# A ScalarE copy that reads PSUM in steps of four tokens and writes them side by side

## The chip, the cores and the metric

The kernel runs on one core of a Trainium2 chip. The metric is the time of one execution on the device, in microseconds (us). A core has five engines that run side by side and wait for each other through semaphores: TensorE (matrix products; in the profile "PE" for matmuls and "PEld" for weight loads, which overlap the matmuls), VectorE ("DVE"), ScalarE ("ACT"), GpSimd ("POOL") and SyncE ("SP", which here issues transfers). Matmuls write to PSUM; the other data lie in SBUF.

## The reference

The network has two layers on an input of shape (8, 256, 32, 32): 8 batches, 256 channels, 1024 tokens (32 x 32 pixels). Everything is fp32.

```
# layer 0: 8 heads of 64, softmax over the queries (axis 1)
xt   = x.reshape(B, C, S).transpose(0, 2, 1)
qkv  = (xt @ w_qkv + b_qkv).reshape(B, S, 8, 3 * 64); q, k, v = split(qkv)
attn = softmax(einsum('bihd,bjhd->bijh', q, k) * 64**-0.5, axis=1)
res  = einsum('bijh,bjhd->bihd', attn, v).reshape(B, S, 512)
t    = res @ w_out + b_out + xt
# layer 1
t = t + attention(layernorm(t), W)              # 1024 x 1024 scores per batch
t = t + top2_of_8_experts(layernorm(t), ...)    # two 256x256 matrices per expert, gelu between
```

The change concerns `res`, the result of layer 0's attention, and the product `res @ w_out`.

## The kernel before

The batches go through the two attentions one after the other. For seven of them the experts' rows are scattered to memory and worked off in blocks afterwards; the last batch goes through all experts densely.

Layer 0 (`layer0`) goes through steps (g, j): g is one of 4 pairs of heads (128 of the 512 inner channels), j one of 8 blocks of 128 keys. In each step TensorE makes scores for two heads (`score`, L468), VectorE takes their maximum (L483, L492), ScalarE takes the exponential and its sum (`soften`, L509), and TensorE multiplies with the values divided by the sums (`gather_values`, L545). It sums all 8 key blocks of a pair into two PSUM banks `po[0]` and `po[1]`, each 128 channels x 512 tokens. With the last key block ScalarE copies both to `res[:, g, :]` in SBUF (L563); `res` has 128 channels on the partitions, then 4 pairs, then 1024 tokens. So there are 8 copies in a batch and 64 in all, always two together. In the steps (0, 3), (1, 1) and (2, 1) TensorE also makes the next pair's queries and keys (`project_pair`, L350), which ScalarE evicts from PSUM (L315); the pair before is finished two steps late (`LAG = 2`), so the copies of pairs 0 and 1 fall beside projections. These copies stand ahead of the evictions L315 on ScalarE, and those of pair 2 ahead of an exp. The pool `ps_acc` has only two buffers, which `po`, `pr` and others take in turn: the next pair's first products wait until the copies have freed them.

After the last step comes the output product: for each of 8 blocks i of 128 tokens, four matmuls over the pairs g add up `pr` (L636), with `res` as the weights that are loaded and `wo` (128 x 256) as what moves; VectorE adds `pr` to the residual `t1` (L639) and the layer norm of layer 1 begins (L235, L236, L238 to L242). As the trace counts, each fp32 matmul is two records, each with its own weight load: 8 x 4 x 2 = 64 records of L636 in a batch, 512 in all. In front of this stage and behind it stand products for the next batch (L328, L387); layer 1's own attention has products of the same shape in L695 (`py`, weights `aT`).

The tokens of a block are not side by side. `NH2` = 2 halves of 512 tokens, each of `NB` = 4 blocks: block i holds the tokens 4p + i of its half, for p from 0 to 127, so that the partition p of a block's tile is the p-th group of four tokens. The function `own` picks a block out of `res` with this step of 4 elements (16 bytes).

The order of the instructions on each engine is set when the program is built, by the order of the code and by `tc.issue_after`; it is the same before and after the change.

Of the kernel before, what the change touches and what calls it, by code (L numbers as in the profile page):

```python
# [19 lines left out]
def kernel(  # L20
# [23 lines left out]
    nc = tc.nc  # L44
    P = 128
    B, C, S = x.shape
# [6 lines left out]
    NH2 = S // 512  # L53
    NPAIR = INNER // P
# [24 lines left out]
    def acc(name):  # L79

        return ps_acc.tile([P, 512], F32, tag="acc", name=name)
# [39 lines left out]
    wo = const.tile([P, NPAIR, C], F32, name="wo")  # L121
# [87 lines left out]
    NB = NT // NH2  # L209
    SQ = 32  # L210
    NQ = P // SQ

    def own(t, i):

        return t.rearrange("c (n p i) -> c n i p", n=NH2, i=NB)[:, i // NB, i % NB, :]

    def bcast(t, n):

# [222 lines left out]
    def layer0(b, xT, begun, routing, xs):  # L441
# [8 lines left out]
        res = one.tile([P, NPAIR, S], F32, tag="res", name=f"res_{b}")  # L450
# [8 lines left out]
        po, copied, counted = None, None, None  # L459
# [73 lines left out]
        def gather_values(at, turn):  # L533


            nonlocal po, copied
            g, j = steps[at]
            if j == 0 and turn == 0:
                po = [acc(f"po_{b}_{g}_{n}") for n in range(NH2)]
            past = dict(turned)  # L540
            for half in range(2):
                keys = ts(half, DK)
                n = (half + turn) % 2
                for h in range(2):
                    mm = nc.tensor.matmul(  # L545
                        po[n][ts(h, DK), :],
                        vss[at][keys, h, :],
                        exps[at, h][keys, ts(n, 512)],
                        start=(j == 0 and turn == 0),
                        stop=(j == NT - 1 and turn == 1),  # L550
                    )
                    if h == 0 and (j > 0 or turn > 0):
                        tc.add_manual_dep(mm.ins, past[1 - half].ins.name, BEHIND)

                turned[half] = relay.nop()
                tc.add_manual_dep(turned[half].ins, mm.ins.name, BEHIND)
            if turn == 0:
                return mm
            vss.pop(at)
            for h in range(2):  # L560
                exps.pop((at, h))
            if j == NT - 1:
                copied = [nc.scalar.copy(res[:, g, ts(n, 512)], po[n]) for n in range(NH2)]  # L563
            return mm

        last = len(steps) - 1
# [7 lines left out]
        for at in range(last + LAG + 1):  # L574
            g, j = steps[min(at, last)]
# [10 lines left out]
            if at >= LAG:  # L586
                with tc.issue_after(counted.ins) if counted else nullcontext():
                    gather_values(at - LAG, 0)
                counted = None
# [18 lines left out]
            if at >= LAG:  # L608
                array = gather_values(at - LAG, 1)
# [23 lines left out]
        for i in range(NT):  # L633
            pr = acc(f"pr_{b}_{i}")
            for g in range(NPAIR):
                nc.tensor.matmul(  # L636
                    pr[:, :C], own(res[:, g, :], i), wo[:, g, :], start=(g == 0), stop=(g == NPAIR - 1)
                )
            nc.vector.tensor_add(t1[:, i, :], pr[:, :C], t1[:, i, :])  # L639
        return t1  # L640
# [675 lines left out]
    for b in range(B):  # L1316
        xT = next_x
        if b + 1 < B:
            next_x = load_x(b + 1)
        if b > 0:  # L1320
            xs = load_squares(b)
        t1 = layer0(b, xT, begun, routing, xs)
        if b + 1 < B:
            begun = Begin(b + 1, next_x)
            t2 = attend(b, t1, begun.at)
            n2, _, l = normed(b, t2, begun.at)
            nc.sync.dma_start(groups[0].sums[b], t2)
            routing = dispatch(b, n2, l, groups[0])
            continue
        experts(groups[0])  # L1330
        others = Results(groups[0])
        others.begin()
        norm = None

        def fill(place):

            nonlocal norm
            others.tick(place)
            if place == "last products":
                norm = Norm(t1, one.tile([P, NT, D], F32, tag="xa", name=f"n2_{b}"), 1e-5, f"f{b}")  # L1340
                return norm.blocks(0, NT - 1)

        t2 = attend(b, t1, fill, others.tick)
        dense(b, t2, norm, others.tick)
        assert others.added == len(others.units) and not others.whole
# [42 lines left out]
```

## Time and profile before

| | us |
|---|---|
| runs of the kernel (three) | 2415.96, 2416.36, 2419.54 |
| median | 2416.36 |
| the profiled execution, its own time | 2397.03 |
| span in its profile (first to last instruction) | 2395.3 |
| TensorE matmuls busy, of the span | 2353.9 |
| ScalarE busy, of the span | 938.0 |
| L636 matmuls / weight loads, busy | 121.6 / 120.7 |
| L563 copies, busy | 34.2 |

The granted clock of TensorE was 0.996 of full speed. In the profile "L563" is a line of the kernel; a group of instructions is given as out<-in, with its shape (partitions x elements), its number, its busy time together, the mean ns of one, and the idle time of the engine just before with what ended it. Matmuls are pipelined, so the duration of a single one is longer than its share of the time; the distance from one start to the next says what it costs. Durations come from one profiled execution, which took 2397.03 us, 0.8% less than the median of the runs.

### The profile page before, as it was taken

The page shows a single profiled execution, that of the slowest core. Times are in us where ns is not written, and L with a number is a line of the kernel's source. Part 1 is how long each engine was busy: PE and PEld are TensorE (multiplying, and loading weights), DVE is VectorE, ACT ScalarE, POOL GpSimd, SP SyncE. Part 2 cuts the span into 40 slices and gives each one's busy share as a digit, 9 for nine tenths or more (in the row PEclk, how much of TensorE's full clock was granted, in tenths as well). Part 3 has the DMA queues.
Part 4 walks back from the last instruction along what each step waited for, and adds up shares of the span by engine and source line. Part 5 has one row for each costly group of instructions (what it writes and reads, how often), then busy time and mean ns, then how long its engine had stood idle before and what let it go on. Part 6 is the DMA issues. An engine that isn't in the chain of part 4 may idle for free.

```text
span 2395.3 us, 36813 instructions
## 1 busy us (share of the span) xinstructions
PE 2353.9 (98%) x13759; PEld 1313.9 (55%) x13759; DVE 1541.2 (64%) x3660; ACT 938.0 (39%) x1570; POOL 420.4 (18%) x391
## 2 busy tenths in 40 slices
PE   9999999999999999999999999999999999999898
PEld 3356534654466336633664356435653388887565
DVE  5775587457845785578647864787468763334776
ACT  3651266126611662156315641465136612221111
POOL 0000012000200020003000200020002234444663
PEclk9999999999999999999999999999999999999999
DMA  8993201010101010001000100100010256664454
GB/s 294 386 386 106 53 19 36 1 36 12 43 1 36 8 47 1 18 18 54 1 18 18 47 8 3 34 25 12 1 36 19 76 176 220 219 215 162 148 172 119
DMA packets 114778, 196.59 MB, mean 82 GB/s; under 512 B 15752, under 2 KB 58408, under 8 KB 112808
## 3 DMA queue, kind: packets, MB, share of 16 engines
q1 hardware_dynamic: 88504, 126.52, 16.0%
q0 software_dynamic: 25008, 67.20, 9.1%
q8 instruction: 109, 1.79, 0.3%
q10 hardware_dynamic: 1088, 0.52, 0.1%
q14 instruction: 69, 0.57, 0.1%
HBM read 108.88 MB, written 110.90 MB: 92 GB/s over the span
## 4 chain that ended last, share of the span: by engine, by line
PE 90%; DVE 5%; DMA 2%; ACT 1%; issue 1%; POOL 0%; SPq 0%; DVEq 0%; ACTq 0%; POOLq 0%
PE po L545 19%; PE psc L468 18%; PE py L695 8%; PE ps L670 7%; PE pqk L350 7%; PE pr L636 5%; PE pv L387 4%; PE ph L1025 4%; PE pe L1050 4%; PE pdh L1254 2%; PE px L655 2%; PE pdy L1278 2%; PE pa L689 2%; PE pqk L328 2%; PE px L1015 1%
## 5 line engine op out<-in xcount | busy, mean ns | idle before, releaser
L509 ACT ACTIVATE ex<-psc,nmax 128x1024 f32<-128x1024 f32 x512 | 570.5, 1115 | 304.1 <-DVE scrap L492 220.4
L468 PE MATMUL psc<-qk,qk 64*64 64x512 f32 x4096 | 577.4, 593 | 10.3 <-ACT ex L509 10.3
L545 PE MATMUL po<-ex,vs 64*64 64x512 f32 x4096 | 573.2, 592 | 1.3 <-DVE vs L525 0.3
L492 DVE TENSOR_SCALAR_CACHE_REDUCE scrap<-psc,nmax 128x512 f32<-128x512 f32 x512 | 384.5, 751 | 149.0 <-PE psc L468 121.8
L483 DVE TENSOR_REDUCE nmax<-psc 128x1 f32<-128x512 f32 x512 | 350.7, 685 | 9.3 <-PE psc L468 9.3
L468 PEld LDWEIGHTS psc<-qk,qk 64*64 64x64 f32 x4096 | 180.7, 132 | 285.9 <-ACT ex L509 138.3
L545 PEld LDWEIGHTS po<-ex,vs 64*64 64x64 f32 x4096 | 177.6, 132 | 273.0 <-issue 81.2
L695 PE MATMUL py<-n,aT 128*128 128x256 f32 x1024 | 236.3, 384 | 2.9 <-DVE aT L691 2.9
L670 PE MATMUL ps<-nT,xa 128*128 128x512 f32 x512 | 236.0, 592 | 0.0
L695 PEld LDWEIGHTS py<-n,aT 128*128 128x128 f32 x1024 | 190.5, 190 | 66.1 <-DVE aT L691 41.8
L888 POOL DMA_INDIRECT rows<-n,d_at x112 | 108.8, 972 | 654.4 <-DVE nmax L483 654.1
L681 ACT ACTIVATE ex<-ps,nmax 128x1024 f32<-128x1024 f32 x64 | 71.3, 1115 | 348.0 <-DVE nmax L678 333.5
L815 POOL TENSOR_TENSOR t<-t,n 128x2048 f32<-128x2048 f32 x8 | 36.3, 4532 | 924.0 <-DVE n L242 924.0
L350 PE MATMUL pqk<-xT,wqkv 128*128 128x512 f32 x384 | 171.2, 599 | 0.0
L701 DVE SCALAR_TENSOR_TENSOR t<-py,rs,t 128x256 f32<-128x256 f32 x64 | 30.9, 483 | 192.7 <-PE py L695 192.7
L670 PEld LDWEIGHTS ps<-nT,xa 128*128 128x128 f32 x512 | 93.5, 190 | 81.2 <-issue 75.1
L350 PEld LDWEIGHTS pqk<-xT,wqkv 128*128 128x128 f32 x384 | 71.0, 190 | 99.9 <-issue 77.8
L1134 POOL DMA_INDIRECT yk<-y,yat x112 | 111.0, 991 | 70.1 <-issue 27.1
L636 PEld LDWEIGHTS pr<-wo,res 128*128 128x128 f32 x512 | 120.7, 331 | 3.7 <-ACT res L563 3.7
L636 PE MATMUL pr<-wo,res 128*128 128x256 f32 x512 | 121.6, 398 | 0.3 <-ACT res L563 0.3
L387 PE MATMUL pv<-wqkv,xT 128*128 128x512 f32 x256 | 120.3, 599 | 1.2 <-DVE v L395 1.0
L315 ACT ACTIVATE qk<-pqk,b_qks 128x512 f32<-128x512 f32 x124 | 85.6, 691 | 88.9 <-PE pqk L350 79.8
(189 smaller groups left out, 2477.8 us busy)
## 6 DMA issues: line engine op xcount, KB each, us to landing
rows<-wb SPq DMA_DIRECT2D x7, 8192.0 KB, 51.7
y<-yb SPq DMA_DIRECT2D x63, 256.0 KB, 2.3
xs<-in_x_dram SPq DMA_DIRECT2D x64, 128.0 KB, 4.0
out_dram<-oT SPq DMA_DIRECT2D x60, 128.0 KB, 2.9
xT<-in_x_dram SPq DMA_DIRECT2D x7, 1024.0 KB, 4.8
sums<-t SPq DMA_DIRECT2D x7, 1024.0 KB, 3.9
o<-sums SPq DMA_DIRECT2D x7, 1024.0 KB
wpack<-in_L_ffn_w_dram SPq DMA_DIRECT2D x4, 1024.0 KB
```

Of the source, the lines that this page charges most:

```text
L350: mm = nc.tensor.matmul(pq[:, ts(n, 512)], wqkv[:, cc, t, ts(g, P)], xT[:, cc, ts(n, 512)], start=(cc == 0), stop=(cc == NCC - 1),)
L387: nc.tensor.matmul(pv, self.xT[:, cc, ts(i, P)], wqkv[:, cc, 2, :], start=(cc == 0), stop=(cc == NCC - 1),)
L468: mm = nc.tensor.matmul(pss[at, h][ts(c, DK), ts(n, 512)], k[r, j * P + c * DK : j * P + (c + 1) * DK], q[r, ts(n, 512)], start=True, stop ...
L483: firsts[at, h] = nc.vector.tensor_reduce(nmax, pss[at, h][:, ts(0, 512)], AX.X, ALU.max, negate=True)
L492: seconds[h] = nc.vector.tensor_scalar(scrap, pss[at, h][:, ts(1, 512)], -1.0, nmaxes[at, h], ALU.mult, ALU.min, accum_out=nmax,)
L509: nc.scalar.activation(ex, pss.pop((at, h)), AF.Exp, bias=nmaxes.pop((at, h)), scale=1.0, accum_out=sums[at][:, h : h + 1],)
L545: mm = nc.tensor.matmul(po[n][ts(h, DK), :], vss[at][keys, h, :], exps[at, h][keys, ts(n, 512)], start=(j == 0 and turn == 0), stop=(j == ...
L636: nc.tensor.matmul(pr[:, :C], own(res[:, g, :], i), wo[:, g, :], start=(g == 0), stop=(g == NPAIR - 1))
L670: nc.tensor.matmul(psc[:, ts(n, 512)], xa[:, ec, ts(i, P)], nT[:, ec, ts(n, 512)], start=(ec == 0), stop=(ec == NCC - 1),)
L695: nc.tensor.matmul(py[:, :D], aT[:, ts(m, P)], n1[:, m, :], start=(m == 0), stop=(m == NT - 1))
L888: scatter = nc.gpsimd.indirect_dma_start(out=view[:, :], out_offset=bass.IndirectOffsetOnAxis(ap=ats[k][:, i : i + 1], axis=0), in_=n2[:, ...
L1134: ins = nc.gpsimd.indirect_dma_start(out=self.slot(at)[:, k, :], out_offset=None, in_=self.group.y[:, :], in_offset=bass.IndirectOffsetOnAxis(
```

## The change

The copy out of PSUM reorders the tokens: it goes over the four blocks i of its half and for each over p, so it reads `po` with a step of 4 elements and writes each block's 128 tokens side by side in `res`. The output product then takes a contiguous slice, and `own` is gone. What is computed stays the same.

```diff
-    def own(t, i):
-
-        return t.rearrange("c (n p i) -> c n i p", n=NH2, i=NB)[:, i // NB, i % NB, :]
-
...
             if j == NT - 1:
-                copied = [nc.scalar.copy(res[:, g, ts(n, 512)], po[n]) for n in range(NH2)]
+
+                copied = [
+                    nc.scalar.copy(
+                        res[:, g, ts(n, 512)].rearrange("c (i p) -> c i p", i=NB),
+                        po[n].rearrange("c (p i) -> c i p", i=NB),
+                    )
+                    for n in range(NH2)
+                ]
             return mm
...
                 nc.tensor.matmul(
-                    pr[:, :C], own(res[:, g, :], i), wo[:, g, :], start=(g == 0), stop=(g == NPAIR - 1)
+                    pr[:, :C], res[:, g, ts(i, P)], wo[:, g, :], start=(g == 0), stop=(g == NPAIR - 1)
                 )
```

## The prediction

> **What bounds the kernel now.** I read the engine totals first, then the chain of waits, then the groups of instructions with their shapes kept apart, and last the timeline around each place where `res` is written and read. From the page:
>
> ```profile
> PE 2353.9 (98%) x13759; PEld 1313.9 (55%) x13759; DVE 1541.2 (64%) x3660; ACT 938.0 (39%) x1570; POOL 420.4 (18%) x391
> ...
> PE po L545 19%; PE psc L468 18%; PE py L695 8%; PE ps L670 7%; PE pqk L350 7%; PE pr L636 5%; PE pv L387 4%; PE ph L1025 4%; PE pe L1050 4%; PE pdh L1254 2%; PE px L655 2%; PE pdy L1278 2%; PE pa L689 2%; PE pqk L328 2%; PE px L1015 1%
> ```
>
> TensorE is on the chain 90% of the span, so a microsecond saved or lost on it counts in full unless a wait follows. The reader of `res`, L636, is 5% of the chain. ScalarE, which writes `res`, is only 39% busy. But share of busy time says little about where its lateness is felt. The groups by shape:
>
> ```profile
> L695 PEld LDWEIGHTS py<-n,aT 128*128 128x128 f32 x1024 | 190.5, 190 | 66.1 <-DVE aT L691 41.8 <-issue 0.2
> L636 PEld LDWEIGHTS pr<-wo,res 128*128 128x128 f32 x512 | 120.7, 331 | 3.7 <-ACT res L563 3.7
> L563 ACT COPY res<-po 128x512 f32<-128x512 f32 x64 | 34.2, 588 | 28.9 <-PE po L545 28.9
> ```
>
> The same weight load, 128 rows by 128 columns in fp32, takes 331 ns for `res` and 190 ns for `aT`. The only difference I find is the step between columns: `own` picks every fourth fp32 (16 bytes), `aT` is contiguous. A load overlaps a matmul, so its duration is not its price; the price is the distance from one matmul to the next. Timeline of both stages (columns: start us, length us):
>
> ```profile
> 168.50 15.09 PEld L636 LDWEIGHTS pr<-wo,res 128*128 128x128 f32 x64 [0.45 <-ACT res L563]
> 168.72 15.18 PE L636 MATMUL pr<-wo,res 128*128 128x256 f32 x64
> ...
> 183.73 1.88 PE L328 MATMUL pqk<-xT,wqkv 128*128 128x512 f32 x4
> ...
> 207.90 3.62 PE L695 MATMUL py<-n,aT 128*128 128x256 f32 x16
> 211.14 0.41 PEld L670 LDWEIGHTS ps<-nT,xa 128*128 128x128 f32 x2
> 211.35 1.88 PE L670 MATMUL ps<-nT,xa 128*128 128x512 f32 x4
> ```
>
> From the first matmul of a stage to the first of the next: L636 (183.73 - 168.72)/64 = 0.2345 us a record, L695 (211.35 - 207.90)/16 = 0.2156 us. Both move 256 columns with 128x128 weights. So L636 runs 19 ns a record slower than the same shape elsewhere, and in L636 the loads touch end to end (15.09 us for 64): they are the limit there.
>
> [...] no row of this trace shows ScalarE reading PSUM with a step. [...] the trace has 588, and its slope, (1115 - 691)/512 = 0.83 ns between the L509 and L315 rows[...].
>
> **The change part by part.** Both programs have the same instructions in the same order on all five queues, with the same waits. Two access patterns differ.
>
> (1) The weight loads of L636 become contiguous. I take their pace as 0.2156 us instead of 0.2345: 64 x 0.0189 = 1.21 us in each of 8 batches, 9.7 us. All of it is on TensorE. It reaches the end if nothing behind it is late: VectorE adds each `pr` (L639, 0.42), then L235 and L236 (0.43, 0.18), about 1.1 us a block with its gaps, against 8 x 0.2156 = 1.72 us of matmuls per block, so VectorE keeps up. After the last block L238 to L242 follow, covered by L328 and L387 until the transposes; they hang on the last matmul and move with it. ScalarE's L315 and table load (168.92 to 170.9) are done long before. So 9.7 us, at worst a few tenths a batch less.
>
> (2) The 64 copies of L563 read PSUM with a step of 16 bytes, in four runs of 128, and write contiguously. Call what each takes longer d. Three places feel it:
>
> ```profile
> 140.10 1.07 ACT L563 COPY res<-po 128x512 f32<-128x512 f32 x2 [0.35 <-PE po L545]
> ...
> 140.73 0.19 PEld L545 LDWEIGHTS po<-ex,vs 64*64 64x64 f32 x4 [0.70 <-ACT res L563]
> ...
> 141.06 1.13 ACT L509 ACTIVATE ex<-psc,nmax 128x1024 f32<-128x1024 f32 x1
> ...
> 141.22 0.14 PEld L545 LDWEIGHTS po<-ex,vs 64*64 64x64 f32 x2 [0.29 <-ACT res L563]
> ```
>
> Head pair 2 (8 times): the loads for the next `po` wait for both copies, one after the other, and the exp L509 is queued behind them. The second copy is 2d late: 16d in all. Head pair 3 (8 times): the first load of L636 (168.50) starts 0.05 us after the first copy (168.45), and its matmul at 168.72 follows L328 without a gap. No slack: 8d. The second copy is needed only by the fourth product, six records or 1.3 us later, so it costs nothing more. Head pairs 0 and 1 (16 times): queued behind the copies is the eviction L315 of the projection, and the load of its third half-product waits for that:
>
> ```profile
> 71.82 1.06 ACT L563 COPY res<-po 128x512 f32<-128x512 f32 x2
> ...
> 72.76 0.71 ACT L315 ACTIVATE qk<-pqk,b_qks 128x512 f32<-128x512 f32 x1
> ...
> 73.72 0.19 PEld L350 LDWEIGHTS pqk<-xT,wqkv 128*128 128x128 f32 x1 [0.24 <-ACT qk L315]
> ```
>
> The eviction ends at 73.47. The load serves the matmul due at 74.15 and takes 0.19, so it could start near 73.95: about 0.43 us of slack after the 0.05 of the semaphore. Cost 16 x max(0, 2d - 0.43). In sum the change loses 24d + 16 x max(0, 2d - 0.43), and breaks even with 9.7 us at d = 0.30 us.
>
> The trace does not show d, so I bound it. It can't be below nothing in any amount that counts: the elements and the engine are the same, and the writes were contiguous before. Upper end: [...]512 x 0.83 = 0.43 us, a copy of 1.01 us. Nearest rows, on VectorE: L842 copies 64 elements read with a step of 32 bytes in 209 ns, against 194 for the contiguous 63 of L949, nearly nothing; L853 writes 64 with that step in 275 against 225 for L854, 50/64 = 0.8 ns more per element. So it is the write and the weight load that pay in this trace, and here the step is on a read, from PSUM[...]. I take d = 0.01 us, for the four runs instead of one: cost 24 x 0.01 = 0.24 us.
>
> Sum: -9.7 + 0.2 = -9.5 us. Against the profiled execution's own time (2397.03 us, span 2395.3) this is 2387.5; the runs' median is 2416.36, and I subtract the same: 2406.9 us.
>
> **The rivals.** (A, forecast, chance 0.52) d under 0.1 us: 2405 to 2411.
>
> (B, slower, 0.29) ScalarE reads a 16-byte step in PSUM at half rate. For it: the doubled step penalty of the weight loads, STREAM_TRANSPOSE L434, which reads `xs` with a 16-byte step at 2060/1024 = 2.0 ns an element[...]. Against it: L842. d = 0.43: 24 x 0.43 + 16 x 0.43 = 17.2 us lost, 9.7 gained, +7.5: 2423.9 us. It decides from d = 0.30 us, copies of about 890 ns, and is clearly slower from 0.39.
>
> (C, 0.12) A part penalty[...] (L853 paid 0.8 ns on VectorE): 512 x 0.42 ns, d = 0.21, loss 5.0, net -4.7: 2411.7 us; between d = 0.2 and 0.39 nothing measurable.
>
> (D, 0.07) The loads are not what paces L636, so the change doesn't do what it says; or VectorE's chain after it takes the gain back. For it: the matmul rows differ a little too (398 ns for L636, 384 for L695). Against it: the loads that touch end to end. About 2416.6 us.
>
> **How the numbers follow.** This kernel's runs spread over 3.6 us, so 0.2% (4.8 us) is about what can be told from no change. Faster: A and the low part of C, 0.54. Slower: B and the top of C, 0.30. Same: the rest of C and D, 0.16. The range goes from 2405 (A with d nothing and half a microsecond more from the stage's first load and its neighbours, less noise) to 2424.5 (B); the likeliest case alone has 2405 to 2411.
>
> **What would show it.** The L636 loads at about 190 ns and the stage at 13.8 us instead of 15.0 show step 1; loads still over 300 ns, or 15.0 us, refute it. L563's mean of 588 ns shows d: under 620 is A, near 800 C, near 1010 B. In B the loads of `po` after head pair 2 and the third projection product wait longer for ScalarE, and TensorE's idle before L545, L350 and L636 grows.

## The result, and the profile after

| kernel | median us | runs |
|---|---|---|
| before | 2416.16 | 2415.09 to 2419.54, 6 runs |
| changed | 2407.95 | 2403.03 to 2410.94, 6 runs |

The ratio is 0.9963, with a 95% interval of 0.995 to 0.9975: 8.2 us less in the medians, between 6 and 12 us less by the interval. The forecast was 2406.9 us and a gain of 9.5 us.

The groups by shape of the changed kernel (L639 is the line that was L636 before, L561 the one that was L563):

```profile
L639 PE MATMUL pr<-wo,res 128*128 128x256 f32 x512 | 111.9, 379 | 0.3 <-ACT res L561 0.3
L639 PEld LDWEIGHTS pr<-wo,res 128*128 128x128 f32 x512 | 97.2, 190 | 16.7 <-ACT res L561 3.7
L561 ACT COPY res<-po 128x512 f32<-128x512 f32 x64 | 34.2, 588 | 28.8 <-PE po L541 28.8
```

The loads fell from 331 to 190 ns and are no longer busy from end to end (97.2 us, 16.7 idle in front of them). The copies take 588 ns, to the nanosecond what they took when they read PSUM in order. The timeline of the stage in batch 0 (start us, length us):

```profile
167.92 1.07 ACT L561 COPY res<-po 128x512 f32<-128x512 f32 x2 [3.21 <-PE po L541]
168.55 13.79 PEld L639 LDWEIGHTS pr<-wo,res 128*128 128x128 f32 x64 [0.45 <-ACT res L561]
168.77 13.98 PE L639 MATMUL pr<-wo,res 128*128 128x256 f32 x64
...
182.58 1.88 PE L324 MATMUL pqk<-xT,wqkv 128*128 128x512 f32 x4
```

(182.58 - 168.77)/64 = 0.2158 us a record; it was 0.2345. Matched matmul by matmul, the two traces drift apart by 1.2 us within each of the stages of batches 0 to 6 and by nothing between them. By the end of batch 6's stage the changed kernel is 8.4 us ahead. In batch 7 it loses about 1.1 us in this profile before its own output stage, and 8.5 us remain behind that stage.

One thing misleads at first sight: this profiled execution took 2410.6 us, more than the 2397.03 of the profile before. The two ends can't be compared: 2410.6 us is one of the six runs of the changed kernel, but 2397.03 us is none of the six runs of the kernel before, which took at least 2415.09 us. And the difference lies behind the part that changed. Busy time by stretches, first of the changed kernel, then of before; the second column is the stretch's length, the next are engines (TensorE, its loads, VectorE, ScalarE, GpSimd), and then come the granted clock and the transfers:

```profile
0.00:1900.00 1900.00, 1881.84 (x11665) 932.55 (x11669) 1283.57 (x3135) 841.48 (x1377) 187.55 (x158) 1.00 0.18 58
1900.00:2150.00 250.00, 243.85 (x1247) 207.77 (x1240) 102.74 (x227) 54.55 (x125) 112.15 (x114) 1.00 0.63 203
2150.00:2409.00 259.00, 231.31 (x852) 156.48 (x851) 154.37 (x300) 42.00 (x69) 120.87 (x119) 0.92 0.47 137
```

```profile
0.00:1907.20 1907.20, 1889.17 (x11665) 954.99 (x11669) 1283.58 (x3135) 841.51 (x1377) 187.12 (x158) 1.00 0.18 58
1907.20:2157.00 249.80, 244.06 (x1243) 209.84 (x1235) 102.12 (x226) 54.53 (x125) 111.28 (x114) 1.00 0.62 203
2157.00:2395.40 238.40, 220.64 (x858) 149.12 (x856) 155.53 (x300) 41.99 (x69) 121.96 (x120) 0.97 0.51 149
```

Up to 1900 us the changed kernel has issued as many matmuls (11,665) as the other up to 1907.2. In the last stretch, the last batch's second layer, its clock was 0.92 against 0.97, and the same work took about 20 us longer. Whether that belongs to the change is decided by the repeated run e6 below.

### The profile page after: what moved, and what is told of

It is laid out like the page before. It is cut to its first block, busy times and chain, and to the rows that moved or that the text cites. A ratio compares the mean times of both kernels' runs of the same rounds, so it can differ in the third digit from the quotient of the medians.

```text
span 2408.9 us, 36813 instructions
## 1 busy us (share of the span) xinstructions
PE 2357.0 (98%) x13759; PEld 1296.8 (54%) x13759; DVE 1540.7 (64%) x3660; ACT 938.0 (39%) x1570; POOL 420.6 (17%) x391
## 4 chain that ended last, share of the span: by engine, by line
PE 89%; DVE 5%; issue 1%; ACT 1%; DMA 1%; POOL 1%; another core or an unknown queue 1%; SPq 0%; DVEq 0%; ACTq 0%; POOLq 0%
PE po L541 19%; PE psc L464 18%; PE py L698 9%; PE ps L673 7%; PE pqk L346 7%; PE pr L639 5%; PE ph L1028 4%; PE pv L383 4%; PE pe L1053 4%; PE px L658 2%; PE pdh L1257 2%; PE pdy L1281 2%; PE pa L692 2%; PE pqk L324 2%; PE px L1018 1%
## 5 line engine op out<-in xcount | busy, mean ns | idle before, releaser
L698 PE MATMUL py<-n,aT 128*128 128x256 f32 x1024 | 242.3, 391 | 6.8 <-DVE aT L694 4.2
L681 DVE TENSOR_REDUCE nmax<-ps 128x1 f32<-128x1024 f32 x64 | 78.1, 1220 | 59.0 <-PE ps L673 59.0
L639 PE MATMUL pr<-wo,res 128*128 128x256 f32 x512 | 111.9, 379 | 0.3 <-ACT res L561 0.3
```

The source lines that it names most:

```text
L639: nc.tensor.matmul(pr[:, :C], res[:, g, ts(i, P)], wo[:, g, :], start=(g == 0), stop=(g == NPAIR - 1))
L698: nc.tensor.matmul(py[:, :D], aT[:, ts(m, P)], n1[:, m, :], start=(m == 0), stop=(m == NT - 1))
```

## The experiments

The first four ran on one chip, the next four on another; each is compared with the kernel before on its own chip (medians 2399.17 us, 27 runs, and 2399.06 us, 9 runs). In the result above the kernel before had a median of 2416.16 us; which chip that was is not recorded. The changed kernel itself did not run on the first of these chips; there e1 stands for it. e7, e8 and e9 are single runs, made for the durations in their profiles.

**e1: only the loads change.** The copy of before, and the product takes contiguous slices, so the tokens meet the residual in another order.

```diff
-                    pr[:, :C], own(res[:, g, :], i), wo[:, g, :], start=(g == 0), stop=(g == NPAIR - 1)
+                    pr[:, :C], res[:, g, ts(i, P)], wo[:, g, :], start=(g == 0), stop=(g == NPAIR - 1)
```

> The copy is the contiguous one of the kernel before; only the weight loads of the output product are contiguous (the product then takes tokens in another order than the residual's, so the output rows are permuted). Theory A (the whole change is the pace of the loads; the copy's step is free): loads 190 ns, the stage of 64 records 13.8 us, time as with the full change, 2407 to 2408 us. Rival R (the loads gain more, and the stepped copy gives a part back): below 2404 us.

Measured: 2389.34 us (5 runs), ratio 0.9958 [0.9945, 0.9971], 9.8 us less. Groups by shape:

```profile
L636 PEld LDWEIGHTS pr<-wo,res 128*128 128x128 f32 x512 | 97.2, 190 | 16.7 <-ACT res L563 3.7
L563 ACT COPY res<-po 128x512 f32<-128x512 f32 x64 | 34.2, 588 | 28.9 <-PE po L545 28.9
```

The expectation's 2407 us counts from the 2416 us of the result above; it is the difference that counts, and it is that of theory A.

**e2: only the copy changes.** The copy of the changed kernel, and `own` stays.

```diff
-                copied = [nc.scalar.copy(res[:, g, ts(n, 512)], po[n]) for n in range(NH2)]
+                copied = [
+                    nc.scalar.copy(
+                        res[:, g, ts(n, 512)].rearrange("c (i p) -> c i p", i=NB),
+                        po[n].rearrange("c (p i) -> c i p", i=NB),
+                    )
+                    for n in range(NH2)
+                ]
```

> The copy reads PSUM with a step of 4 elements as in the changed kernel, and the product still takes its weights with a step of 4 (so the tokens of a half are permuted twice). Theory A: copies 588 ns, loads 331 ns, stage 15.0 us, time as before, 2416 us. Rival R: copies above 620 ns and slower than before; by the prediction's sum 24 d + 16 max(0, 2 d - 0.43), for d = 0.43 us 2433 us.

Measured: 2399.07 us (14 runs), ratio 1.0001 [0.9993, 1.0009]. Groups by shape:

```profile
L642 PEld LDWEIGHTS pr<-wo,res 128*128 128x128 f32 x512 | 120.7, 331 | 3.7 <-ACT res L564 3.7
L564 ACT COPY res<-po 128x512 f32<-128x512 f32 x64 | 34.2, 588 | 28.9 <-PE po L545 28.9
```

The step costs the copy nothing, and the loads, which still have theirs, keep the 331 ns. Rival R is out: the change is the sum of a gain of 9.8 us (e1) and of nothing (e2, within about 2 us by its interval).

**e3: the step on the copy's other side.** Same layout of `res` and same result, but the copy goes through PSUM in order and writes SBUF with a step of 128 elements.

```diff
-                        res[:, g, ts(n, 512)].rearrange("c (i p) -> c i p", i=NB),
-                        po[n].rearrange("c (p i) -> c i p", i=NB),
+                        res[:, g, ts(n, 512)].rearrange("c (i p) -> c p i", i=NB),
+                        po[n].rearrange("c (p i) -> c p i", i=NB),
```

> The same layout of res as in the changed kernel, but the copy goes through PSUM in order and writes SBUF with a step of 128 elements instead of reading PSUM with a step of 4. Theory A1 ([...]whatever the step on either side): copies 588 ns, time as with the change, 2408 us. Theory A2 (it is the side in SBUF that pays, as on VectorE in L853 and on the weight loads): copies about 1010 ns, d = 0.43, loss 17.2 against 9.7 gained, 2424 us.

Measured: 2402.16 us (13 runs), ratio 1.0007 [0.9999, 1.0015] to before, and 12.8 us above e1. The group, and the places where it is felt:

```profile
L561 ACT COPY res<-po 128x512 f32<-128x512 f32 x64 | 62.2, 1075 | 28.9 <-PE po L541 28.9
```

```profile
71.80 1.93 ACT L561 COPY res<-po 128x512 f32<-128x512 f32 x2
...
73.51 1.51 ACT L311 ACTIVATE qk<-pqk,b_qks 128x512 f32<-128x512 f32 x2
74.26 0.30 PEld L346 LDWEIGHTS pqk<-xT,wqkv 128*128 128x128 f32 x2 [0.79 <-ACT qk L311]
...
140.58 1.95 ACT L561 COPY res<-po 128x512 f32<-128x512 f32 x2 [0.35 <-PE po L541]
141.68 0.20 PEld L541 LDWEIGHTS po<-ex,vs 64*64 64x64 f32 x4 [1.16 <-ACT res L561]
...
142.58 0.14 PEld L541 LDWEIGHTS po<-ex,vs 64*64 64x64 f32 x2 [0.71 <-ACT res L561]
...
169.10 1.92 ACT L561 COPY res<-po 128x512 f32<-128x512 f32 x2 [3.22 <-PE po L541]
170.19 1.38 PEld L639 LDWEIGHTS pr<-wo,res 128*128 128x128 f32 x7 [0.90 <-ACT res L561]
170.19 1.56 PE L639 MATMUL pr<-wo,res 128*128 128x256 f32 x6
```

Theory A2 is right on the mechanism: the step on the SBUF side makes the copy 1.8 times as long. One copy takes 0.49 us longer on average, but two in a row take 1.93 us instead of 1.06, so d = 0.43 us for each of a pair, which is the d of the prediction's rival B. That makes e3 a test of the prediction's price for a slow copy, with the same instruction order as the changed kernel. The waits appear where they were forecast, but they are smaller. In batch 0, from the delay of the same matmuls against e1 (the sum takes batch 0 times eight):

| head pair | forecast us, d = 0.43 | measured us |
|---|---|---|
| 0 | 2d - 0.43 = 0.43 | 0.23 |
| 1 | 0.43 | 0.27 |
| 2 | 2d = 0.86 | 0.75 |
| 3 | d = 0.43 | 0.34 |
| sum, 8 batches | 17.2 | 12.7 |

**e5: every copy twice.** The changed kernel with one line more in the list, so that each copy is issued twice in a row; the exponential that was placed behind both copies is now placed behind the second copy of each half.

```diff
                     for n in range(NH2)
+                    for _ in range(2)
                 ]
...
-                with tc.issue_after(copied[0].ins), tc.issue_after(copied[1].ins):
+                with tc.issue_after(copied[1].ins), tc.issue_after(copied[3].ins):
                     soften(at, 0)
```

> The changed kernel with every copy issued twice in a row, so that each po is released about 0.48 us later (d = 0.48, as two copies overlap by 0.1 us). It prices a slow copy, which the prediction's rival B rests on. Prediction's sum: 24 x 0.48 + 16 x (0.96 - 0.43) = 20 us over the changed kernel, 2428 us. Rival H (other work hides most of it, as TensorE waits anyway in these places): less than 8 us over the changed kernel.

Measured: 2419.26 us (5 runs), ratio 1.0081 [1.0068, 1.0094], 29.9 us above e1 and not 20. It is not a clean price, for two reasons that its trace shows. In head pairs 0 to 2 the second copy of a tile starts only when the first has ended, so four take 2.30 us instead of 1.06 for two, and d is 0.62 (in head pair 3 they overlap and take 2.05). And the build, which sets the order, put other work in another order; which of the two edited lines led to that was not tried. The timeline after the output product:

```profile
186.83 0.69 ACT L311 ACTIVATE qk<-pqk,b_qks 128x512 f32<-128x512 f32 x1 [13.96 <-PE pqk L324]
187.54 1.28 ACT L235 ACT_TABLE_LOAD   x1
188.83 0.21 ACT L235 ACTIVATE rstd_a<-rstd_a 128x8 f32<-128x8 f32 x1
...
189.85 0.44 PE L256 MATMUL pt_n<-ident,n 128*128 128x128 f32 x2 [1.34 <-DVE n L238]
```

The table load of the layer norm, which ran at 169.62 beside the output product before, now stands behind an eviction and in front of the norm, and TensorE waits 1.34 us for the norm. In batch 0 head pairs 0 to 2 cost 2.6 us against e1, and this place 1.5, of which 0.2 is won back soon after. Head pair 3 costs nothing here, because two more matmul records of a projection (L324) stand ahead of the output product in this build. Rival H is out: head pairs 0 to 2 alone cost about 21 us in 8 batches, not under 8.

**e6: the changed kernel again**, unaltered, beside the last three.

> The changed kernel unaltered, on a chip together with the next three. If the loads are the whole change it stands 9.6 us below the kernel before, as the run with the loads alone did (9.8 us there), and the last batch's half-clock stretches differ from run to run. If the stepped copy costs something, it stands less than 8 us below.

Measured: 2389.97 us (5 runs), ratio 0.996 [0.9946, 0.9974], 9.1 us less than before. Its last stretch, by the same view as above:

```profile
1900.00:2150.00 250.00, 244.46 (x1246) 208.64 (x1242) 102.25 (x225) 54.03 (x123) 111.87 (x114) 1.00 0.63 204
2150.00:2390.00 240.00, 220.43 (x849) 148.87 (x847) 155.03 (x299) 41.95 (x69) 121.33 (x119) 0.96 0.51 148
```

Here the last stretch took 238 us to the end of the span (2388.1) at a clock of 0.96, with the same code that took 259 us at 0.92 in the first profile. So the loss there does not belong to the change. It belongs to that execution or to where it ran: in the result both kernels' medians stand 17 to 18 us above those of this chip, and the six runs of the changed kernel there had a mean clock of 0.990 to 0.994, against 0.993 to 0.995 for the five here. In the first profile TensorE's granted clock was 0.50 in six stretches of 3.4 or 6.8 us between 2150 us and the last few us, and in e6 in three of 3.4 us; it was also idle there for 28 us against 18. In the 5 us ahead of each of the six it had been idle for 1.21 to 3.65 us at a time, but ahead of one of e6's three it had not been idle at all. So idle time alone does not explain them, and what sets one off was not tried.

**e7: a step of 2 elements.** The copy writes SBUF with a step of 2 and the loads read with a step of 2 (another order of tokens than the reference's, as in e8 and e9).

```diff
-                copied = [nc.scalar.copy(res[:, g, ts(n, 512)], po[n]) for n in range(NH2)]
+                copied = [
+                    nc.scalar.copy(res[:, g, ts(n, 512)].rearrange("c (p i) -> c i p", i=2), po[n].rearrange("c (i p) -> c i p", i=2))
+                    for n in range(NH2)
+                ]
...
-                    pr[:, :C], own(res[:, g, :], i), wo[:, g, :], start=(g == 0), stop=(g == NPAIR - 1)
+                    pr[:, :C], res[:, g, :].rearrange("c (n p i) -> c n i p", n=4, i=2)[:, i // 2, i % 2, :], wo[:, g, :], start=(g == 0), stop=(g == NPAIR - 1)
```

> Weight loads with a step of 2 elements (8 bytes), copies that read PSUM in order and write SBUF with a step of 2 (tokens in another order than the reference's). Theory L[...]: loads 190 ns and copies 588 ns. Theory S (any step halves the rate on the SBUF side): loads 331 ns and copies about 1050 ns.

```profile
L639 PEld LDWEIGHTS pr<-wo,res 128*128 128x128 f32 x512 | 100.3, 196 | 13.7 <-ACT res L564 3.9
L564 ACT COPY res<-po 128x512 f32<-128x512 f32 x64 | 36.0, 621 | 28.8 <-PE po L545 28.8
```

Both pay a little (6 and 33 ns), far from double. The run took 2390.18 us, like the changed kernel, and the loads stand idle again (13.7 us): at 8 bytes they no longer pace the stage.

**e8: PSUM read with a step of 128 elements, loads with a step of 8.**

```diff
-                copied = [nc.scalar.copy(res[:, g, ts(n, 512)], po[n]) for n in range(NH2)]
+                copied = [
+                    nc.scalar.copy(res[:, g, ts(n, 512)].rearrange("c (p i) -> c p i", i=NB), po[n].rearrange("c (i p) -> c p i", i=NB))
+                    for n in range(NH2)
+                ]
...
-                    pr[:, :C], own(res[:, g, :], i), wo[:, g, :], start=(g == 0), stop=(g == NPAIR - 1)
+                    pr[:, :C], res[:, g, :].rearrange("c (p i) -> c i p", i=8)[:, i, :], wo[:, g, :], start=(g == 0), stop=(g == NPAIR - 1)
```

> Copies that read PSUM with a step of 128 elements (512 bytes) and write SBUF in order; weight loads with a step of 8 elements (32 bytes); tokens in another order than the reference's. Theory P ([...]at any step): copies 588 ns. Rival (a step of 16 bytes is still near enough, a far one is not): over 900 ns. Loads: 331 ns as at 16 bytes[...]; more than 400 ns if the distance counts.

```profile
L639 PEld LDWEIGHTS pr<-wo,res 128*128 128x128 f32 x512 | 123.0, 336 | 3.7 <-ACT res L564 3.7
L564 ACT COPY res<-po 128x512 f32<-128x512 f32 x64 | 34.2, 587 | 28.9 <-PE po L545 28.9
```

Theory P's number came: 587 ns even at 512 bytes. The loads are about as slow at 32 bytes (336 ns) as at 16 (331), and the run took 2398.68 us, like the kernel before.

**e9: SBUF written with a step of 4 elements**, contiguous loads. Against the changed kernel, whose contiguous loads stay:

```diff
                 copied = [
-                    nc.scalar.copy(
-                        res[:, g, ts(n, 512)].rearrange("c (i p) -> c i p", i=NB),
-                        po[n].rearrange("c (p i) -> c i p", i=NB),
-                    )
+                    nc.scalar.copy(res[:, g, ts(n, 512)].rearrange("c (p i) -> c i p", i=NB), po[n].rearrange("c (i p) -> c i p", i=NB))
                     for n in range(NH2)
                 ]
```

> Copies that read PSUM in order and write SBUF with a step of 4 elements (16 bytes), contiguous weight loads; tokens in another order than the reference's. Theory L: about 1075 ns, as with the step of 128 elements (e3)[...]. Rival: 588 ns, only far steps are slow.

```profile
L564 ACT COPY res<-po 128x512 f32<-128x512 f32 x64 | 63.9, 1105 | 28.9 <-PE po L545 28.9
```

A copy takes 1105 ns with a step of 16 bytes, 1075 with 512 (e3), 621 with 8 and 588 in order; the run took 2405.27 us, slower than the kernel before's 2399.06, as e3 was in its median. So the jump lies between 8 and 16 bytes, and at 512 bytes the copy takes no longer than at 16. What makes the jump was not shown. ScalarE's reads of PSUM have none: 588, 588 and 587 ns with steps of 4, 16 and 512 bytes.

## Why the prediction was right

*Step 1, the loads.* Forecast: 0.2156 us a record, 9.7 us. Measured: 0.2158 us, and 9.8 us with the loads alone (e1). What made the number good was to read the pace from a stage of the same shape, not the duration of a load: 331 - 190 = 141 ns times 512 would have been 72 us. That VectorE keeps up (each `pr` is added in 0.42 us, and in batch 0 VectorE then stood idle for 0.55 to 0.62 us until the next one) and the norm moves with the last matmul held in every batch; none of the gain was given back before batch 7.

*Step 2, the copy.* Taken was d = 0.01 us, the low end of 0 to 0.43; it is 0.00 (588 ns in both profiles, and e2). The reasons were half right. The rows that spoke for rival B (STREAM_TRANSPOSE, the weight loads) all had their step in SBUF, where e3 and e9 show that ScalarE's writes pay too (1075 and 1105 ns against 588); none had it in PSUM. The loads' penalty, called doubled, was 331 against 190 ns, 1.7 times. The sizes of d for B and C were the author's estimates, 512 times the measured 0.83 ns (0.43 us) and half of that (0.21); the 0.01 us for the four runs had no number behind it. No row of the profile before showed any of the three. For STREAM_TRANSPOSE the trace has no contiguous row to compare, so that its 2.0 ns an element come from the step is not shown. The row that spoke against B (L842) was a read by VectorE from SBUF and said nothing of ScalarE or PSUM. So the profile before could not decide it, and that d came out at the very low end was in part luck.

*Rival B's price.* This is the part that was off. A slow copy does stop TensorE in the places it named, as e3 shows at d = 0.43 us, but the loss was 12.8 us and not 17.2. Most of the difference is in head pairs 0 and 1, where 16 x 0.43 us was forecast and about 0.25 each was measured. Two terms were mis-sized there. The eviction behind the copies ended 0.75 us late in e3 and not 2d = 0.86, because it begins 0.2 us before the end of the second slow copy, and only 0.1 before that of a fast one. And the load was priced at its 0.19 us, although a late load costs less: in e3's profile the matmul of a late load starts with it (both at 170.19 above), and the next matmul follows after 0.53 us instead of 0.43 (0.32 instead of 0.22 in the output product). So it costs 0.10 us, and the slack behind the eviction is 0.52 us, not 0.43. Head pair 3, which was said to have no slack, has 0.1 us for the same reason: its load used to start 0.22 us ahead of its matmul (168.50 and 168.72). With B's copy, by e3, the kernel would have ended 3.0 us above before and not 7.5, which is less than the 4.8 us that the prediction itself called no change. So rival B, listed as the slower case, would not have been clearly slower, and its share in the chance of slower was too high.

*The rest.* Rivals C and D are out by the copies' 588 ns and the stage's 13.8 us. One reading costs nothing but is wrong: in head pair 3 the fourth product of the first block reads the half that the first copy writes; the half of the second copy is first read in block 4. The measured gains (8.2, 9.1, and 9.8 for the loads alone) agree within their intervals with 9.5.

## What to carry to other kernels

Where data must change order between PSUM and SBUF, put the step on ScalarE's PSUM read: for these copies of 128 x 512 fp32 it was free at both steps tried (588 and 587 ns at 16 and 512 bytes, 588 in order), while steps of 16 and 512 bytes in SBUF nearly doubled the copy when ScalarE wrote with them (1105 and 1075 ns), and steps of 16 and 32 bytes slowed TensorE's weight load (331 and 336 ns against 190). ScalarE's reads from SBUF were not tried. A slow weight load costs only as much as it lengthens the distance between matmuls (here 19 ns a record, though each load took 141 ns longer), so compare that distance with a stage of the same shape. And compare two traces matmul by matmul up to the place of the change: the ends of two executions can differ by more than the change is worth (here by about 20 us in the last stretch, against a gain of 8 to 10).

## What the runs showed of the hardware

ScalarE's copy of 512 fp32 took 588 ns reading PSUM in order, 588 with a step of 16 bytes and 587 with 512 bytes. Writing SBUF it took 621 ns with a step of 8 bytes, 1105 with 16 and 1075 with 512. A 128x128 fp32 weight load took 190, 196, 331 and 336 ns with steps of 4, 8, 16 and 32 bytes, and with the last two it set the pace of 256-column matmuls, as the loads stood idle for only 3.7 us of the execution against 16.7 and 13.7 with the first two: 0.2345 us at 16 bytes and, from e8's timeline, (183.86 - 168.56)/64 = 0.2391 at 32, instead of 0.2158. Not expected was that a weight load that a late semaphore releases holds up the row of matmuls by only 0.10 us, although it takes 0.19, and that the same two programs took 17 to 18 us longer in the median in the result's runs than on the chips of the experiments. In the one profile of those runs, that of the changed kernel, the extra time lies in the last stretch; its cause stays open.
